# A decoder layer on one core: its last block set apart, the second batch's first chunk normalised earlier, and load buffers divided

## The chip, the cores and the metric

The kernel runs on one core of one Trainium2 chip. The metric is the device time of one execution in microseconds (us), the median of several runs; less is better. The engines are called as in the profile: PE (TensorE, matmuls; PEld its weight loads), DVE (VectorE), ACT (ScalarE), POOL (GpSimd) and SP (SyncE), whose queue here issues all DMAs.

## The reference

Two sequences (B = 2) of 2048 rows and 512 columns go through one decoder layer, in float32:

```python
x = x + _L0_attn_ref(_layernorm(x), W_q, W_k, W_v, W_o)   # 16 heads of 32, rotary positions on Q and K, softmax
x = x + _L0_xattn_ref(_layernorm(x), ctx, ctx)            # gelu(x @ ctx.T) @ ctx, ctx is 77 x 512
x = x + _L0_ffn_ref(_layernorm(x), weights, scale, bias)  # sign(weights), scale, bias, clip to +-100
```

The layer norms have no learned parameters. The attention is over all 2048 keys.

## The kernel before

The rows of a sequence are cut into 16 chunks of 128 rows; four chunks are a block of 512. For each batch two stages follow one another.

**Projection** (`project_batch`). For each chunk the rows are loaded (`load_x`, L69), normalised (`norm`: statistics on DVE, L129 and L130; four small operations on POOL, L135 to L139; the normalised `xn` on ACT, L155), transposed on PE and copied (`turn`: `pt` L161, `xnt` L163), and multiplied by three weights (`pk`, `pq`, `pv`, L168). K and Q are rotated on DVE (L196 to L200) and POOL (L201) and transposed again (`ptqk`, L176). The loop works one chunk ahead: in the round of chunk ch, `norm(ch + 1)` is issued, and its load was issued two chunks ahead. The x tiles of the projection and of the work behind the attention share one pool of six buffers (`xpool`).

**Attention** (`Attention.run`). A unit is a group of four heads with 256 queries; there are 32 units (`NU`) of 8 steps (`STEPS`) in a batch. Each step has two half-steps of two heads each: scores (`st`, L496), exponentials on ACT (`pw`, L623), their pairwise sum on POOL (`sm`, L625). In between come the weighing of the values (`acc`, L514) and the sums (L528) for the step before, and the maxima of the scores for a unit ahead (`ps` L403 on PE, L415 on DVE). The queries' maxima enter the scores as a row `mrow` (L481). `divide` (L542 to L551) ends a unit. Keys are kept as differences from one block to the next; the differences `dk` lie in the buffers of the three projection weights, so that the next batch's weights (`load_qkv`, L74) can be loaded only when the last scores have read them.

**Background.** When a block of queries is done, `divide` puts a generator `after_attention` on a queue. It does the rest of the layer for its chunks: output projection (`po`, L309) and addition to x (L285), normalisation (L292, `xn` L297, transposes `pt` L303), the product with the context (`ph` L316), gelu (L318 to L330), the product back (`po`, L335), normalisation, and the last product (`pf`, L343) with scale, bias, clip, addition and store (L345 to L352). At each `yield` it gives back control and says whether the next piece is heavy, which mostly means matmuls. `background(n)` runs n pieces; with `light=True` it stops ahead of a heavy one. It is called once or twice in each attention step and twice, with three pieces, for each chunk of the projection. The last block of queries is handed over in two halves of two chunks. In batch 1 the second half has one generator for each chunk, and these run when the attention is over, with DVE in POOL's place (`side`).

**Order.** Inside `run`, `tc.manual_schedule` keeps PE, DVE, ACT and POOL in the order in which the program is written. Elsewhere, and for SP everywhere, a scheduler orders the instructions by readiness and place in the program. Each engine and SP's queue then runs in order.

Of the kernel before, what the change touches and what calls it, by code (L numbers as in the profile page):

```python
# [9 lines left out]
F32 = mybir.dt.float32  # L10
# [25 lines left out]
def decoder_layer(  # L36
# [17 lines left out]

    const = ctx.enter_context(tc.tile_pool(name="const", bufs=1))
    kvq = ctx.enter_context(tc.tile_pool(name="kvq", bufs=1))
    xpool = ctx.enter_context(tc.tile_pool(name="xpool", bufs=6))
    big = ctx.enter_context(tc.tile_pool(name="big", bufs=3))
    sums = ctx.enter_context(tc.tile_pool(name="sums", bufs=3))
    work = ctx.enter_context(tc.tile_pool(name="work", bufs=5))  # L60
# [3 lines left out]
    ps_acc = ctx.enter_context(tc.tile_pool(name="ps_acc", bufs=1, space=bass.MemoryType.PSUM))  # L64


    def load_x(b, ch):
        t = xpool.tile([P, D], F32, tag="x", name=f"x_{b}_{ch}")
        nc.sync.dma_start(t, x[b, ch * P : (ch + 1) * P, :])  # L69
        return t  # L70

# [58 lines left out]
        nc.vector.bn_aggr(mv, st)  # L130


    def scale_and_shift(engine, mv, n):
        y = small.tile([P, n], F32, tag=f"rstd{n}", name="rstd")
        engine.tensor_scalar(y, mv[:, :, 1], EPS, None, ALU.add)  # L135
        nc.gpsimd.tensor_tensor(y, y, minus_half[:, :n], ALU.pow)
        off = small.tile([P, n], F32, tag=f"off{n}", name="off")
        engine.tensor_mul(off, mv[:, :, 0], y)
        engine.tensor_scalar(off, off, -1.0, None, ALU.mult)  # L139
        return y, off  # L140

    def project_batch(b, ahead, att, wk, wq, wv):

        def norm(ch):
            xc = ahead.pop(0)
            if ch + 2 < NCH:
                ahead.append(load_x(b, ch + 2))  # L150
            mv = small.tile([P, 1, 2], F32, tag="mv1", name="mv")
            chunk_stats(xc, mv[:, 0])
            y, off = scale_and_shift(nc.gpsimd, mv, 1)
            xn = work.tile([P, D], F32, tag="w", name="xn")
            nc.scalar.activation(xn, xc, AF.Identity, bias=off, scale=y)  # L155
            return xn

        def turn(xn):
            pt = ps_t.tile([P, ND, P], F32, tag="t", name="pt")
            for i in range(ND):  # L160
                nc.tensor.transpose(pt[:, i, :], xn[:, i * P : (i + 1) * P], ident)  # L161
            xnt = work.tile([P, ND, P], F32, tag="w", name="xnt")
            nc.scalar.copy(xnt, pt)  # L163
            return xnt

        def times(dst, xnt, w, part=range(ND)):
            for i in part:
                nc.tensor.matmul(dst, xnt[:, i, :], w[:, i, :], start=(i == 0), stop=(i == ND - 1))  # L168
# [31 lines left out]
            nc.vector.tensor_tensor(t2[:, :, :, 1], pairs[:, :, :, 0], sn, ALU.mult)  # L200
            nc.gpsimd.tensor_add(r[:, 0, a], r[:, 0, a], r[:, 1, a])  # L201

        xnt = turn(norm(0))
        held = None
        for ch in range(NCH):
            if ch == (NB - 1) * CPB:
                drain()
            blk, c = divmod(ch, CPB)
            if c == 0:
                att.q.append(kvq.tile([P, ND, BLK], F32, tag=f"q{blk}", name=f"q_{b}_{blk}"))  # L210
                att.k.append(kvq.tile([P, ND, BLK], F32, tag=f"k{blk}", name=f"k_{b}_{blk}"))
            r = big.tile([P, 2, 2, D], F32, tag="s", name="r")
            xn = norm(ch + 1) if ch + 1 < NCH else None
            pk = ps_t.tile([P, D], F32, tag="t", name="pk")
            pq = ps_t.tile([P, D], F32, tag="t", name="pq")
            if ch == NCH - 1:
                break
            times(pk, xnt, wk)
            rotate(ch, 1, pk, r)
            att.lead(1)  # L220
            background(3)
            times(pq, xnt, wq)
            rotate(ch, 0, pq, r)
            if held is not None:
                transpose_qk(*held)
            held = (ch, r[:, 0])
            xnt_next = turn(xn)
            if ch < NCH - 2:
                values(ch, xnt)
            else:  # L230
                left = xnt
            att.lead(1)
            background(3)
            xnt = xnt_next


# [31 lines left out]
        return ps_t.tile(shape, F32, tag="t", name=name)  # L268


    def after_attention(b, blk, ot, first, end):
        wo, wf, fs, fb = late["wo"], late["wf"], late["fs"], late["fb"]
        ctxn, ctxt = late["ctx"]
        n = end - first
        chunks = [slice(c * P, (c + 1) * P) for c in range(first, end)]
        whole = slice(first * P, end * P)
        xs = [load_x(b, blk * CPB + c) for c in range(first, end)]
        yield True


        def add_to_x(matmuls, mv):
            for c in range(n):
                ps = bank([P, D], "po")
                matmuls(ps, chunks[c])
                nc.vector.tensor_add(xs[c], ps, xs[c])  # L285
                yield False
                chunk_stats(xs[c], mv[:, c, :])
                yield c + 1 < n


        def norm(mv):
            y, off = scale_and_shift(side(), mv, n)  # L292
            yield False
            yield False
            for c in range(n):
                xn = work.tile([P, D], F32, tag="w", name="xn2")
                nc.scalar.activation(  # L297
                    xn, xs[c], AF.Identity, bias=off[:, c : c + 1], scale=y[:, c : c + 1]
                )
                yield True  # L300
                pt = bank([P, ND, P], "pt2")
                for i in range(ND):
                    nc.tensor.transpose(pt[:, i, :], xn[:, i * P : (i + 1) * P], ident)  # L303
                nc.scalar.copy(ot[:, :, chunks[c]], pt)
                yield c + 1 == n
# [2 lines left out]
            for i in range(ND):  # L308
                nc.tensor.matmul(ps, ot[:, i, cols], wo[:, i, :], start=(i == 0), stop=(i == ND - 1))  # L309

        mv = small.tile([P, n, 2], F32, tag=f"mv{n}", name="mv2")
        yield from add_to_x(project_out, mv)
        yield from norm(mv)
        ph = bank([C, n * P], "ph")
        for i in range(ND):
            nc.tensor.matmul(ph, ctxt[:, i, :], ot[:, i, whole], start=(i == 0), stop=(i == ND - 1))  # L316
        h = work.tile([C, n * P], F32, tag="w", name="h")
        nc.scalar.copy(h, ph)  # L318
        yield False
        u = work.tile([C, n * P], F32, tag="w", name="u")  # L320
        side().tensor_mul(u, h, h)
        yield False
        side().tensor_scalar(u, u, 0.044715, 1.0, ALU.mult, ALU.add)
# [10 lines left out]
        def attend_ctx(ps, cols):  # L334
            nc.tensor.matmul(ps, u[:, cols.start - whole.start : cols.stop - whole.start], ctxn, start=True, stop=True)  # L335

        mv = small.tile([P, n, 2], F32, tag=f"mv{n}", name="mv3")
        yield from add_to_x(attend_ctx, mv)
        yield from norm(mv)
        for c, cols in enumerate(chunks):  # L340
            pf = bank([P, D], "pf")
            for i in range(ND):
                nc.tensor.matmul(pf, ot[:, i, cols], wf[:, i, :], start=(i == 0), stop=(i == ND - 1))  # L343
            y = work.tile([P, D], F32, tag="w", name="y")
            nc.vector.tensor_mul(y, pf, fs)  # L345
            yield False
            side().tensor_add(y, y, fb)
            yield False
            side().tensor_scalar(y, y, -MAX_VAL, MAX_VAL, ALU.max, ALU.min)
            side().tensor_add(xs[c], xs[c], y)  # L350
            r0 = blk * BLK + (first + c) * P
            nc.sync.dma_start(out[b, r0 : r0 + P, :], xs[c])  # L352
            yield True

    queue = []
    heavy = [False]

    def background(n, light=False):  # L360
        while queue and n > 0 and not (light and heavy[0]):
            more = next(queue[0], queue)
            if more is queue:
                queue.pop(0)
                heavy[0] = False
            else:
                heavy[0] = more
                n -= 1

    def drain():  # L370
        while queue:
# [5 lines left out]
    class Attention:  # L377
# [160 lines left out]
        def divide(self, u):  # L538
# [16 lines left out]
                )  # L555
            if g == ND - 1 and (hf == 1 or qb == NB - 1):
                first = hf * (CPB // 2) if qb == NB - 1 else 0
                size = 1 if last else (hf + 1) * (CPB // 2) - first
                for c in range(first, (hf + 1) * (CPB // 2), size):
                    queue.append(after_attention(self.b, qb, self.q[qb], c, c + size))  # L560


        def open_block(self, kb):
# [11 lines left out]
        def run(self):  # L575
# [33 lines left out]
            )  # L609
            ordered.__enter__()  # L610
            attending.append(True)
            for t in range(NU * STEPS):
                u, i = divmod(t, STEPS)
                pw = big.tile([P, 4, 2, HQ], F32, tag="s", name="pw")
                sm = sums.tile([P, 4, HQ], F32, tag="sm", name="sm")
                for heads, others in (((0, 1), (2, 3)), ((2, 3), (0, 1))):
# [18 lines left out]
                    else:  # L635
# [6 lines left out]
                            self.turn_maxima(u + 1)  # L642
                        background(1)
                prev = (u, i, pw, sm)
            first_half()
            second_half()
            while ends:
                finish()
            attending.clear()
            ordered.__exit__(None, None, None)  # L650

    for b in range(B):
        att = Attention(b)
        project_batch(b, x_next, att, *qkv)
        if b == 0:
            late_loads()
        load_ctx(b)
        att.run()
        if b + 1 < B:
            x_next = [load_x(b + 1, 0), load_x(b + 1, 1)]  # L660
            qkv = load_qkv()
    alone.append(True)
    while queue:
        for piece in list(queue):
            if next(piece, queue) is queue:
# [47 lines left out]
```

## Time and profile before

| | |
|---|---|
| median of 3 runs | 2783.71 us (2783.66 to 2784.01) |
| the profiled execution, its own time | 2784.56 us |
| its span in the profile | 2782.8 us |
| mean granted clock of PE | 0.996 |
| busy: PE, DVE, ACT, POOL | 99%, 60%, 47%, 63% of the span |

The profile is of one execution. Its span is what the trace covers; the execution's own time is 1.8 us longer. A row of instructions gives line, engine, operation, output and inputs; behind the bar stand busy time, mean duration and idle time ahead with what ended it. A row of waits gives who waited for whom, the total, the number of times and the longest. In a timeline the columns are start and duration in us, then the instruction; matmuls in float32 count as two each.

### The profile page before, as it was taken

To read this page: it belongs to the slowest core of one execution; us is meant where nothing else is said; L and a number is where in the kernel's file an instruction comes from. 1 tells how busy PE (TensorE), PEld (TensorE's weight loads), DVE (VectorE), ACT (ScalarE), POOL (GpSimd) and SP (SyncE) were. 2 spreads that over 40 slices of the span, in tenths; PEclk is the share of its full clock that TensorE was granted. 3 is DMA by queue.
4 is the path that set the end of the run, shared out by engine and by line. 5 is a ranking of instruction groups with operands and counts; after the bars stand their busy time and mean duration, and the time that the engine had idled before them with its cause. 6 is when DMAs were issued, how large, how long until landed. Compare 5 with 4: busy or idle time off the path is not lost.

```text
span 2782.8 us, 70154 instructions
## 1 busy us (share of the span) xinstructions
PE 2750.7 (99%) x30748; PEld 1491.3 (54%) x30748; DVE 1675.7 (60%) x2792; ACT 1320.4 (47%) x2391; POOL 1756.4 (63%) x1903
## 2 busy tenths in 40 slices
PE   8999999999999999999999999999999999999997
PEld 4445555555555555555444455555555555555554
DVE  3436777676666666665234367766757666666652
ACT  2114555455545554654321155555555455545552
POOL 3226767567756685777542277766777567756764
PEclk9999999999999999999999999999999999999999
DMA  4000000000000000000210000000000000000000
GB/s 141 19 16 2 5 4 4 4 4 19 19 4 4 10 27 3 4 19 18 69 31 27 15 4 4 4 4 4 4 24 14 4 4 15 22 3 4 22 7 16
DMA packets 41858, 43.52 MB, mean 16 GB/s; under 512 B 24758, under 2 KB 24758, under 8 KB 41552
## 3 DMA queue, kind: packets, MB, share of 16 engines
q1 hardware_dynamic: 41552, 39.05, 4.7%
q8 instruction: 240, 3.93, 0.6%
q14 instruction: 66, 0.54, 0.1%
HBM read 26.58 MB, written 8.39 MB: 13 GB/s over the span
## 4 chain that ended last, share of the span: by engine, by line
PE 97%; POOL 1%; DVE 1%; DMA 0%; ACT 0%; issue 0%; ACTq 0%; POOLq 0%; DVEq 0%
PE st L496 22%; PE acc L514 22%; PE ps L403 18%; PE acc L528 8%; PE po L309 4%; PE pf L343 4%; PE pq L168 4%; PE pk L168 4%; PE pv L168 4%; PE st L481 3%; PE pt L303 1%; PE po L335 1%; PE ph L316 1%; PE ptqk L176 1%; PE pt L161 1%
## 5 line engine op out<-in xcount | busy, mean ns | idle before, releaser
L625 POOL TENSOR_TENSOR sm<-pw 128x512 f32<-128x512 f32 x1024 | 1296.6, 1271 | 634.5 <-ACT pw L623 631.8
L415 DVE TENSOR_REDUCE mx<-ps 128x1 f32<-128x512 f32 x2048 | 1310.3, 681 | 582.0 <-PE ps L403 579.5
L623 ACT ACTIVATE pw<-st 128x512 f32<-128x512 f32 x2048 | 1111.8, 595 | 1001.8 <-PE ps L403 668.8
L403 PE MATMUL ps<-k,q 32*128 32x512 f32 x4096 | 1208.8, 640 | 1.6 <-DVE mx L415 1.6
L514 PE MATMUL acc<-pw,v 128*32 128x256 f32 x8192 | 655.6, 391 | 0.0
L528 PE MATMUL acc<-sm,ones 128*32 128x128 f32 x7680 | 389.0, 280 | 0.0
L403 PEld LDWEIGHTS ps<-k,q 32*128 32x128 f32 x4096 | 355.3, 183 | 37.7 <-issue 25.8
L514 PEld LDWEIGHTS acc<-pw,v 128*32 128x32 f32 x8192 | 162.4, 108 | 396.3 <-issue 376.6
L528 PEld LDWEIGHTS acc<-sm,ones 128*32 128x32 f32 x7680 | 247.4, 110 | 153.9
L496 PE MATMUL st<-q,dkk 32*128 32x256 f32 x2048 | 291.1, 400 | 0.0
L496 PE MATMUL st<-q,dkq 32*128 32x256 f32 x2048 | 289.9, 400 | 0.0
L496 PE MATMUL st<-q,dkv 32*128 32x256 f32 x2048 | 289.9, 400 | 0.0
L496 PE MATMUL st<-q,k 32*128 32x256 f32 x2048 | 262.8, 374 | 0.0
L201 POOL TENSOR_TENSOR r<-r 128x512 f32<-128x512 f32 x64 | 82.1, 1282 | 246.6 <-DVE r L200 246.3
L496 PEld LDWEIGHTS st<-q,dkk 32*128 32x128 f32 x2048 | 175.4, 184 | 93.2 <-issue 52.3
L496 PEld LDWEIGHTS st<-q,dkq 32*128 32x128 f32 x2048 | 172.7, 184 | 82.6 <-issue 56.7
L496 PEld LDWEIGHTS st<-q,dkv 32*128 32x128 f32 x2048 | 174.7, 184 | 65.2 <-issue 33.6
L496 PEld LDWEIGHTS st<-q,k 32*128 32x128 f32 x2048 | 195.2, 187 | 14.2
L548 DVE RECIPROCAL num<-num 128x128 f32<-128x128 f32 x128 | 120.2, 941 | 60.8 <-ACT num L542 60.8
L177 ACT COPY q<-ptqk 128x512 f32<-128x512 f32 x32 | 18.8, 587 | 232.5 <-PE ptqk L176 232.5
L168 PE MATMUL pk<-wk,xnt 128*128 128x512 f32 x256 | 120.7, 615 | 2.7 <-ACT xnt L163 2.7
L168 PE MATMUL pq<-wq,xnt 128*128 128x512 f32 x256 | 120.9, 612 | 0.0
(90 smaller groups left out, 1860.7 us busy)
## 6 DMA issues: line engine op xcount, KB each, us to landing
x<-in_x_dram SPq DMA_DIRECT2D x64, 256.0 KB, 2.7
out_dram<-x SPq DMA_DIRECT2D x32, 256.0 KB, 2.0
wk<-in_wk_t_dram SPq DMA_DIRECT2D x2, 1024.0 KB, 5.5
wq<-in_wq_t_dram SPq DMA_DIRECT2D x2, 1024.0 KB, 10.5
wv<-in_wv_t_dram SPq DMA_DIRECT2D x2, 1024.0 KB, 9.7
wo<-in_wo_t_dram SPq DMA_DIRECT2D x1, 1024.0 KB
wf<-in_wf_t_dram SPq DMA_DIRECT2D x1, 1024.0 KB, 9.8
mrow<-mt SPq DMA_TRANSPOSE x62, 2.3
```

The costliest lines, as they stand in the source:

```text
L168: nc.tensor.matmul(dst, xnt[:, i, :], w[:, i, :], start=(i == 0), stop=(i == ND - 1))
L309: nc.tensor.matmul(ps, ot[:, i, cols], wo[:, i, :], start=(i == 0), stop=(i == ND - 1))
L343: nc.tensor.matmul(pf, ot[:, i, cols], wf[:, i, :], start=(i == 0), stop=(i == ND - 1))
L403: nc.tensor.matmul(ps, self.q[qb][self.rows[h], g, q0 : q0 + P], self.k[kb][self.rows[h], g, :], start=True, stop=True,)
L415: nc.vector.tensor_reduce(mx[:, qc, h, kb : kb + 1], ps, AX.X, ALU.max)
L481: nc.tensor.matmul(self.st[h], ones_b[r, :], mrow[r, None, :].to_broadcast([DK, 2, HQ]), start=True, stop=False, skip_group_check=True,)
L496: nc.tensor.matmul(self.st[h][:, c, :], keys[r, g, kc * P : (kc + 1) * P], self.q[qb][r, g, hf * HQ : (hf + 1) * HQ], start=False, stop=Tr ...
L514: nc.tensor.matmul(acc[self.rows[h], 0, :], self.v[self.chunk(i, c)][:, d0 : d0 + DK], pw[:, h, c, :], start=(i == 0 and c == 0), stop=(i ...
L528: nc.tensor.matmul(acc[self.rows[h], 1, part], ones, sm[:, h, part], start=False, stop=(i == STEPS - 1), skip_group_check=True,)
L548: nc.vector.reciprocal(num[:, 1, part], num[:, 1, part])
L623: nc.scalar.activation(pw[:, h], self.st[h], AF.Exp, scale=SCALE)
L625: nc.gpsimd.tensor_add(sm[:, hs, :], pw[:, hs, 0, :], pw[:, hs, 1, :])
```

## The change

1. The x tiles get two pools: `xpool` with two buffers for the projection, `xlate` with four for `after_attention`. In the projection the load of chunk ch + 2 is issued behind the normalisation of chunk ch.
2. `norm` and `turn` are no longer local to `project_batch`. The first chunk of batch 1 is loaded in the last unit of batch 0's attention, normalised at the beginning of the last step but one (step 254 of 0 to 255), and transposed behind the last step, before the last weighing.
3. In the projection, `background(3)` at two places for each chunk becomes `background_between(2)` at three: a heavy piece, if it is due, and then light ones, two pieces in all.
4. In batch 1 all four chunks of the last block of queries get generators of their own. They go to a list `tail`, which is worked through in turn when the attention is over.
5. These take their work tiles from the three weight buffers, cut into twelve slices.
6. Mean, variance, scale and shift of a normalisation lie in one tile of four columns.

```diff
-    xpool = ctx.enter_context(tc.tile_pool(name="xpool", bufs=6))
+    xpool = ctx.enter_context(tc.tile_pool(name="xpool", bufs=2))
+    xlate = ctx.enter_context(tc.tile_pool(name="xlate", bufs=4))
...
+    def scale_and_shift(engine, stats):
+        y, off = stats[:, :, 2], stats[:, :, 3]
+        engine.tensor_scalar(y, stats[:, :, 1], EPS, None, ALU.add)
+        nc.gpsimd.tensor_tensor(y, y, minus_half[:, : stats.shape[1]], ALU.pow)
+        engine.tensor_mul(off, stats[:, :, 0], y)
         engine.tensor_scalar(off, off, -1.0, None, ALU.mult)
...
+    def norm(ahead, b, ch):
+        xc = ahead.pop(0)
+        stats = stats_tile(1)
+        chunk_stats(xc, stats[:, 0, 0:2])
+        y, off = scale_and_shift(nc.gpsimd, stats)
+        xn = work.tile([P, D], F32, tag="w", name="xn")
+        nc.scalar.activation(xn, xc, AF.Identity, bias=off, scale=y)
+        if ch + 2 < NCH:
+            ahead.append(load_x(b, ch + 2))
+        return xn
...
             times(pk, xnt, wk)
             rotate(ch, 1, pk, r)
             att.lead(1)
-            background(3)
+            background_between(2)
             times(pq, xnt, wq)
             rotate(ch, 0, pq, r)
+            background_between(2)
...
             att.lead(1)
-            background(3)
+            background_between(2)
...
+    def work_tile(shape, name):
+        if not alone:
+            return work.tile(shape, F32, tag="w", name=name)
+        if not spare:
+            for n in "kqv":
+                t = const.tile([P, ND, D], F32, tag=f"w{n}", name=f"spare{n}")
+                spare.extend(t[:, i, :] for i in range(ND))
+        t = spare.pop(0)
+        spare.append(t)
+        return t[: shape[0], : shape[1]]
...
-        xs = [load_x(b, blk * CPB + c) for c in range(first, end)]
+        xs = [load_x(b, blk * CPB + c, xlate) for c in range(first, end)]
...
+    def background_between(n):
+        if heavy[0]:
+            background(1)
+            n -= 1
+        background(n, light=True)
...
-                size = 1 if last else (hf + 1) * (CPB // 2) - first
+                late = self.b == B - 1 and qb == NB - 1
+                size = 1 if late else (hf + 1) * (CPB // 2) - first
                 for c in range(first, (hf + 1) * (CPB // 2), size):
-                    queue.append(after_attention(self.b, qb, self.q[qb], c, c + size))
+                    (tail if late else queue).append(
+                        after_attention(self.b, qb, self.q[qb], c, c + size)
+                    )
...
+            more = self.b + 1 < B
             for t in range(NU * STEPS):
                 u, i = divmod(t, STEPS)
+                if more and t == (NU - 1) * STEPS:
+                    self.x_next = [load_x(self.b + 1, 0), load_x(self.b + 1, 1)]
+                if more and t == NU * STEPS - 2:
+                    xn = norm(self.x_next, self.b + 1, 0)
...
+            xnt = turn(xn) if more else None
             first_half()
             second_half()
...
     alone.append(True)
+    queue += tail
     while queue:
         for piece in list(queue):
```

## The prediction

> **What bounds the kernel now.** I read the page's busy shares first, then who PE waited for, then PE's busy time and granted clock in windows of 50 us and less, then the timeline where PE was not full.
>
> ```profile
> PE 2750.7 (99%) x30748; PEld 1491.3 (54%) x30748; DVE 1675.7 (60%) x2792; ACT 1320.4 (47%) x2391; POOL 1756.4 (63%) x1903
> PE pt L161 <- ACT xn L155: 9.5, 2, 8.1
> PE pt L303 <- ACT xn L297: 8.1, 5, 3.6
> PE pk L168 <- ACT xnt L163: 2.7, 4, 0.7
> PE po L335 <- DVE u L330: 2.3, 1, 2.3
> PE ps L403 <- DVE mx L415: 1.6, 1, 1.6
> ```
>
> PE is the bound; it idles 2782.8 - 2750.7 = 32.1 us. By the windows: 8.8 before the first matmul, 2.1 where the projection of batch 1 follows the attention of batch 0 (1363 to 1366), 2.1 at 1380 to 1400, 1.6 at 1466 to 1468, 14.3 after 2750, the rest in pieces below 1.1. Only these, and PE's work itself, can be shortened. Some of the idle stretches also cost clock:
>
> ```profile
> 1466.00:1469.00 3.00, 1.39 (x3) 0.82 0.00 0
> 1469.00:1472.00 3.00, 3.00 (x4) 0.50 0.00 0
> 1363.00:1366.00 3.00, 1.14 (x5) 0.92 1.01 363
> 1366.00:1369.00 3.00, 3.00 (x4) 0.51 0.41 141
> 2760.00:2765.00 5.00, 2.50 (x4) 0.66 0.00 0
> 2765.00:2770.00 5.00, 3.63 (x10) 0.50 0.00 0
> ```
>
> (Columns: window, length, PE busy and count, granted clock, DMA.) After each gap PE runs at half clock for 3 to 5 us.
>
> **A. Last block moved to the end.** Of batch 1's last block, chunks 0 and 1 ran as background of the last four units; now all four chunks run alone. First, what leaves the attention:
>
> ```profile
> 2710.91 1.13 PE L496 MATMUL st<-q,dkk 32*128 32x256 f32 x8
> 2712.54 3.70 PE L343 MATMUL pf<-wf,q 128*128 128x512 f32 x8
> 2716.17 1.13 PE L496 MATMUL st<-q,dkq 32*128 32x256 f32 x8
> 2718.02 1.13 PE L496 MATMUL st<-q,dkq 32*128 32x256 f32 x8
> 2719.87 1.13 PE L496 MATMUL st<-q,dkv 32*128 32x256 f32 x8
> ```
>
> A half-step takes 1.85 us (2716.17 to 2718.02); with a pf in it 5.26 to 5.48 us: the piece costs its full 3.63 (2712.54 to 2716.17). [...] The cadence decides: they aren't free. Pieces by the same reading: 2 po and 2 pf at 3.63, 4 pt at 0.59, ph 1.88, 2 ctx products (L335) at 1.06: 14.5 + 2.4 + 1.9 + 2.1 = 20.9 us leave. POOL (1.27 per half-step), ACT (1.09) and DVE stay below 1.85, so no other engine becomes the bound there.
>
> Second, the end. Before, it runs from 2744.6 (first po) to 2782.8, 38.2 us for two chunks: PE's work, 5.7 us behind the last pf (2777.1: multiply, add, clip, add on DVE 2.6, store 2.0 and the rest) and 8.6 us of holes. After: PE's work per chunk is po 3.54, pt 0.60, ph 1.11, L335 1.06, pt 0.60, pf 3.63 = 10.5 alone; packed, as in the projection where four matmuls take 3.43, about 9.7. I take 10.2, so 40.8 for four. The holes are one chunk's latency: po's end to ph is 5.2 us (add 0.69, statistics 0.69, POOL's power 0.56, xn 0.81, transposes 0.66, copy 0.59 and gaps), ph to L335 2.3 to 4.7, then 5 again. With four chunks, behind the last po stand the others' pt, ph and L335, some 8 us of PE work, which cover 5 us; the last pf waits behind three others (10 us). What cover leaves out: about 1 us before the first pf, and DVE. DVE's work per chunk is 2 adds, 2 statistics, 2 sets of small ones (0.18 + 0.15 + 0.16 + 0.15), 1.3 for the gelu and 2.5 at the end: 7.8, four times 31.3, with reciprocals and gaps some 37 us in the 46 that it has. At 80% its queue makes PE wait; I put holes at 2.5 and lost clock at 1.0. End: 40.8 + 3.5 + 5.7 = 50.0, 11.8 more. **A: -20.9 + 11.8 = -9.1** (end holes between 0 and 9 make it -12.6 to -3.6).
>
> Its DMAs: four loads, four stores. The first two loads move from the background to SP's position behind everything, but into four buffers that block 2 has left (its last pf is at 2635.9), and SP has only two transposes and the stores then, so they land long before 2744. Only the last store is seen, within the 5.7. The twelve slices of the dead weight buffers as work tiles cost nothing (dk's last reader is the last scores, before 2744), nor do statistics, scale and shift in one tile: as many instructions as before, and though the tile is now held until xn is read, so is the x buffer.
>
> **B. Load buffers apart.** At 1466 PE stands for this:
>
> ```profile
> 1460.87 0.34 SPq L352 DMA_DIRECT2D out_dram<-x  x1
> 1462.86 0.81 SPq L69 DMA_DIRECT2D x<-in_x_dram  x2
> 1465.62 1.38 DVE L129 BATCH_NORM_STATS2 st<-x 128x6 f32<-128x512 f32 x2 [2.11 <-DMA x<-in_x_dram]
> 1467.64 1.81 PE L403 MATMUL ps<-k,q 32*128 32x512 f32 x2 [1.61 <-DVE mx L415]
> ```
>
> The projection's x waits for a buffer that a background chunk frees only when its store has landed (1462.86); the statistics then hold DVE, DVE the maxima, these PE's bank: 1.61 us, and the next pq takes 6.29 in the chain instead of 3.43: 2.86 more. With two buffers of its own the load waits for the normalisation of the chunk before instead: ACT's xn, then issue 0.3, landing 2.7, statistics 0.9, POOL 1.2, xn 0.8: 6 us in a period of 11 to 13. Behind the waiting load on SP stand the stores and the other loads, which nobody needs soon. The load can still queue behind a store waiting for POOL, but not for its landing (2.0), more than the 1.61. **B: -4.5** (0 if it is still late).
>
> [...] The gaps of 1.61 here, and of 1.40 and 0.68 at 1363, brought 0.50 and 0.51. [...]
>
> **C. Background spread out** (at most one heavy piece per place, three places per chunk). At 1391.38 PE waits 2.10 for xn of the background, since scale, xn and transposes follow too closely. Now places with 3 to 4 us of matmuls lie between. **C: -2.1** (0 to -2.1). The 34 pieces take 22 places, 7 to 8 chunks; the drain before chunk 12 finds nothing.
>
> **D. First chunk of batch 1 in the first attention.** Moved into step 254: two DVE and four POOL instructions, xn on ACT; then four transposes and a copy before the last weighing; two x loads earlier on SP, a third before the weights. Before, from the end of acc (1362.84) to the end of pk (1370.91) pass 8.1 us, 3.4 of it work, 0.66 transposes. But POOL is late:
>
> ```profile
> 1351.48 1.27 POOL L350 TENSOR_TENSOR x<-x,y 128x512 f32<-128x512 f32 x1
> 1352.71 6.19 POOL L625 TENSOR_TENSOR sm<-pw 128x512 f32<-128x512 f32 x5
> 1354.18 1.09 ACT L623 ACTIVATE pw<-st 128x512 f32<-128x512 f32 x2 [0.82 <-PE st L496]
> ```
>
> Before step 254's exponentials (1354.18) three of the five sums precede in POOL's order, so its four small operations start near 1356.4 and take 1.4; xn ends near 1358.7. ACT runs in order: the exponentials, and PE's next scores behind them, are late by 4.6, of which 1.4 is slack: PE stands about 3 us, acc ends near 1365.9, pk follows at once, ending 1369.3 at full clock or 1371.3 at half. The weights, behind the third x load on SP, land 5.5 us after 1359.1: in time. Bounds: -4.0 (no delay) to +1.5. **D: -0.6**, the middle of the two clocks.
>
> **Sum.** -9.1 - 4.5 - 2.1 - 0.6 = -16.3. The profiled execution: span 2782.8, 1.8 around it, 2784.6, which is 0.9 above the median 2783.7. I subtract from the median: 2767.4.
>
> **Rivals.** (1) Lockstep: the four generators, taken in turn, put the in-order queues in stage order, and each stage waits for its last chunk. End: po 14 + 5.2 + 2.4 + gelu 5 + 1 + 5 + 1.3 + pf 14 + 5.7 = 53.6, and 4 for the clock, 57.6: +19.4, A -1.5, total -8.7: 2775. For: DVE at 80%. Against: before, DVE took chunk 2's chain whole before chunk 3's add. (2) It does not happen: the scheduler pulls the ready chunks back into the attention, as it did with batch 1's first statistics (at 1315, 47 us before their use). Then A is 0: -7.2, 2776.5. Against: no matmul was pulled ahead. (3) Slower: the background was free in PE's shadow[...]. Then the attention gives back nothing, the end costs 11.8, B to D give 7.2: +4.6, 2788. It decides when less than 4.6 of the 20.9 is given back. Against: 3.63 for 3.63. (4) Better: POOL is not late at D and the end packs: -4.0 and -11 with B and C: 2762.
>
> **How the numbers follow.** Main forecast 0.62 (2761 to 2773), lockstep 0.15, pulled back 0.09, free background 0.06, better 0.08. The measurement tells 0.2% (5.6 us, below 2778.1) from no change: faster is 0.62 + 0.08 + 0.12 + 0.05 = 0.87, within 0.07, slower 0.06. The range 2758 to 2777 takes in the better case, most of lockstep and half of (2).
>
> **What would show it.** The last units of batch 1 without pf, their half-steps 1.85; PE from the first lone po to the last pf about 44 us at clock near 1; no PE wait for mx near 1466 and none for L297 near 1391; a PE wait of about 3 us on exponentials near 1357, and none between acc and pk. Wrong: an end above 56 us, or po, pf inside the last unit, or the attention shortened by much less than 20.

## The result, and the profile after

The changed kernel takes 2774.64 us (2772.49 to 2775.69, 7 runs) against 2783.71 (2780.70 to 2784.57, 7 runs): a ratio of 0.9967, with a 95% interval of 0.9956 to 0.9979, so 6 to 12 us less. The profiled execution took 2774.21 us, its span is 2772.1. The forecast was 2767.4, within 2758 to 2777.

The busy shares and the waits of PE after (a row of waits: who waited for whom, total, times, longest):

```profile
PE 2746.3 (99%) x30756; PEld 1493.4 (54%) x30756; DVE 1682.3 (61%) x2820; ACT 1320.7 (48%) x2393; POOL 1745.2 (63%) x1888
PE pt L161 <- ACT xn L153: 8.2, 1, 8.2
PE pt L321 <- ACT sparek L315: 4.9, 3, 4.1
PE st L523 <- ACT pw L658: 3.1, 1, 3.1
PE pk L171 <- ACT xnt L163: 2.0, 3, 0.7
PE acc L555 <- POOL sm L660: 0.6, 1, 0.6
PE po L353 <- DVE sparev L348: 0.5, 1, 0.5
```

Three of the waits of before are gone: those of ps for mx, of the background's pt for xn, and of batch 1's first pt for xn (L161 now waits once, at the start of the program). New ones are there: `st` for the exponentials, 3.1, `acc` for a sum of POOL, 0.6, and `pt` in the end for xn, 4.9 (`sparek` is a work tile of the end). The first two lie in the last steps of batch 0's attention, where before PE waited for nothing.

Where the time went is seen best between points that all kernels share: the first maxima row of batch 0's step 252, batch 1's first pk, the first scores of batch 1's attention, the first po behind the attention, the end of the span. Each is the start of one row in the timeline of PE. Each line is one profiled execution; the same stage of the same program differs by up to 1.8 us between lines (the end with unchanged code: 52.2 to 53.8). Stage lengths in us:

| kernel | step 252 to pk | pk to attention of batch 1 | attention of batch 1 | the end | span |
|---|---|---|---|---|---|
| before | 20.2 | 241.5 | 1137.6 | 38.2 | 2782.8 |
| after | 26.4 | 231.7 | 1116.8 | 52.2 | 2772.1 |
| e1, first chunk back | 20.2 | 233.4 | 1117.3 | 53.8 | 2770.0 |
| e2, at step 250 | 17.5 | 231.8 | 1116.9 | 52.5 | 2766.9 |
| e3, small operations at 250 | 18.7 | 231.8 | 1117.2 | 52.3 | 2765.7 |
| e4, two chunks left out | 20.2 | 239.7 | 1117.4 | 40.1 | 2763.5 |
| e5, end alone | 20.2 | 235.4 | 1116.9 | 52.9 | 2771.0 |
| e6, pools alone | 20.2 | 235.5 | 1137.5 | 38.2 | 2777.9 |
| e7, spread alone | 20.2 | 235.3 | 1137.6 | 38.3 | 2777.8 |
| e8, gelu of the end on POOL | 26.3 | 231.8 | 1116.8 | 57.6 | 2777.1 |
| e9, end staggered | 25.9 | 231.7 | 1116.9 | 51.2 | 2769.8 |
| e10, e3 and staggered | 18.8 | 231.7 | 1116.9 | 51.9 | 2764.5 |
| e11, one tile alone | 20.2 | 235.4 | 1137.8 | 38.6 | 2777.4 |

From before to after: +6.2 up to pk, -9.8 in the projection, -20.8 in the attention, +14.0 at the end, and 0.4 earlier at step 252: -10.7, the difference of the spans. In the first two stages 1.7 us only change places: pk ran at half clock before (5.39 us) and at full clock after (3.70). Counted to the end of pk, the first stage is 4.5 longer and the projection 8.1 shorter.

The stage that went wrong is the first. Around step 254 of batch 0 the timeline after shows, in order:

```profile
1345.36 0.23 POOL L139 TENSOR_SCALAR stats<-stats 128x1 f32<-128x1 f32 x1 [0.41 <-DVE stats L131]
1353.76 3.72 POOL L660 TENSOR_TENSOR sm<-pw 128x512 f32<-128x512 f32 x3
1357.56 0.23 POOL L139 TENSOR_SCALAR stats<-stats 128x1 f32<-128x1 f32 x1
1359.08 0.81 ACT L153 ACTIVATE xn<-x,stats 128x512 f32<-128x512 f32 x1 [6.13 <-POOL stats L142]
1359.80 2.04 ACT L658 ACTIVATE pw<-st 128x512 f32<-128x512 f32 x4
1360.43 2.56 PE L523 MATMUL st<-q,dkv 32*128 32x256 f32 x8 [3.09 <-ACT pw L658]
1371.33 3.70 PE L171 MATMUL pk<-wk,xnt 128*128 128x512 f32 x8
```

Three sums hold POOL until 1357.5, its four small operations follow, xn comes at 1359.08, and the exponentials, for which the scores were long ready, only at 1359.80 (ACT stood 6.13 us). PE waits 3.09. POOL was late for one more reason: a set of small operations already stands at 1345.36 to 1349.31. It must be chunk 1's, since chunk 0's xn waits for the later set. Chunk 1's normalisation stands behind `run` in the program; the scheduler put this part of it here, ahead of chunk 0's, and POOL's sums are 1.5 us later against step 252 than in the kernel before. The windows, cut where the granted clock changes, show what the wait does to the clock (window, length, PE busy and count, granted clock, DMA); the last one is in the end:

```profile
1356.50:1359.92 3.42, 0.84 (x18) 1.00 0.92 264
1359.92:1370.16 10.24, 9.73 (x72) 0.50 0.71 239
2745.73:2752.56 6.83, 3.75 (x17) 0.50 0.00 0
```

From 1359.92 to 1370.16 PE runs at half clock, busy for 9.73 us of it, so that 4.9 us are lost: the two half-steps of step 255, the transposes and the last weighing take about twice their time (scores 2.56 and 2.08 instead of 1.13). pk then starts directly behind acc and at full clock.

The attention gives back what was forecast; its last half-steps keep 1.85, and the end begins with four po at once:

```profile
2713.81 1.13 PE L523 MATMUL st<-q,dkv 32*128 32x256 f32 x8
2715.66 1.13 PE L523 MATMUL st<-q,dkv 32*128 32x256 f32 x8
2719.88 14.00 PE L327 MATMUL po<-wo,q 128*128 128x512 f32 x32
```

(No pf stands among them; a half-step is still 2715.66 - 2713.81 = 1.85.) In the end itself the hole lies between the last context product and the second normalisation of chunk 0 (x_12 in the program):

```profile
2741.69 0.68 DVE L303 TENSOR_TENSOR x<-po,x 128x512 f32<-128x512 f32 x1
2743.83 0.68 DVE L130 BATCH_NORM_STATS2 st<-x 128x6 f32<-128x512 f32 x1
2744.59 0.69 DVE L303 TENSOR_TENSOR x<-po,x 128x512 f32<-128x512 f32 x1
2745.20 0.17 DVE L131 BATCH_NORM_AGGREGATE stats<-st 128x2 f32<-128x6 f32 x1
2748.65 1.12 PE L321 MATMUL pt<-ident,sparek 128*128 128x128 f32 x4 [4.10 <-ACT sparek L315]
2752.55 13.91 PE L361 MATMUL pf<-wf,q 128*128 128x512 f32 x32
```

Chunk 0's addition ends at 2742.4; its statistics start 1.4 us later, behind the gelu and the additions of the others, and the aggregate waits in DVE's order behind the fourth addition (2744.59). DVE has no room in this stretch (window, length, DVE busy and count, granted clock of PE, DMA):

```profile
2737.80:2747.80 10.00, 9.71 (x38) 0.90 0.00 0
```

So two things delay chunk 0: DVE is full, and its order serves the other chunks first.

### The profile page after: what moved, and what is told of

Read it like the earlier page. It is cut to its first block, busy times and chain, and to the rows that moved or that the text cites. A ratio compares the mean times of both kernels' runs of the same rounds, so it can differ in the third digit from the quotient of the medians.

```text
span 2772.1 us, 70180 instructions
## 1 busy us (share of the span) xinstructions
PE 2746.3 (99%) x30756; PEld 1493.4 (54%) x30756; DVE 1682.3 (61%) x2820; ACT 1320.7 (48%) x2393; POOL 1745.2 (63%) x1888
## 4 chain that ended last, share of the span: by engine, by line
PE 98%; DVE 1%; POOL 1%; issue 0%; ACT 0%; DMA 0%; POOLq 0%; ACTq 0%; DVEq 0%
PE st L523 22%; PE acc L541 22%; PE ps L430 18%; PE acc L555 8%; PE pk L171 4%; PE pf L361 4%; PE po L327 4%; PE pq L171 4%; PE pv L171 4%; PE st L508 3%; PE pt L321 1%; PE po L353 1%; PE ptqk L179 1%; PE ph L334 1%; PE pt L161 1%
## 5 line engine op out<-in xcount | busy, mean ns | idle before, releaser
L180 ACT COPY q<-ptqk 128x512 f32<-128x512 f32 x32 | 18.8, 587 | 218.7 <-PE ptqk L179 218.6
```

## The experiments

The theory after the result: the attention returned A's 20.9 us as forecast; the shortfall lies in D, whose late POOL costs more than was taken, and in the end, whose hole is larger than taken. Rivals: the pieces in the attention were partly free; D is harmless and all of the shortfall is in the end; xn in front of the exponentials is harmful wherever it stands. The kernel before was measured again beside the runs, with medians of 2784.46 to 2785.27 us, so the ratios are compared and not the times.

**e4: are the pieces free?** From the kernel before; batch 1's first half block gets no work behind the attention.

```diff
+                if self.b == B - 1 and qb == NB - 1 and hf == 0:
+                    return
                 size = 1 if last else (hf + 1) * (CPB // 2) - first
```

> The kernel before, but with the work behind the attention left out for batch 1's last block, first half (chunks 0 and 1; their rows of the output are not computed). It asks what these pieces cost in the attention. Theory (PE is full, each piece costs its whole time): 20.9 us less, 2763 us. Rival (the pieces were free in PE's shadow[...]): 2780 or more, less than 5 us saved.

Measured 2763.93 us against 2785.27, ratio 0.9924 (0.9910 to 0.9937). The attention of batch 1 is 20.2 us shorter in the trace (1117.4 for 1137.6), and 20.8 in the changed kernel. The pieces cost their whole time; the rival falls. The projection of batch 1 is 1.8 us shorter here than in the kernel before, though its program is the same; a half-clock stretch behind the same wait for mx lasted 3.41 us in place of 6.83 (the windows stand in the last section). That is how much one execution's clock can be worth.

**e1: D undone.** The loads of chunks 0 and 1 and `turn(norm(...))` stand again behind `run`.

```diff
-                if more and t == (NU - 1) * STEPS:
-                    self.x_next = [load_x(self.b + 1, 0), load_x(self.b + 1, 1)]
-                if more and t == NU * STEPS - 2:
-                    xn = norm(self.x_next, self.b + 1, 0)
...
-            xnt = turn(xn) if more else None
...
-        project_batch(b, x_next, att, xnt, *qkv)
+        project_batch(b, x_next, att, turn(norm(x_next, b, 0)), *qkv)
```

> The changed kernel with part D alone undone: batch 1's first chunk is again loaded, normalised and transposed behind batch 0's attention; pools, spread background and the end stay as changed. Theory (D costs 4.4 us by the traces: a PE wait of 3.1 on the exponentials of step 254 and some 10 us at half clock behind it): about 2770 us, 4 to 5 less than the changed kernel, no wait of st for pw, pt waiting 1.4 for xn and pk 0.7 for xnt again. Rival (D is neutral or a gain, and the shortfall against the forecast lies in the end): 2774 to 2779.

Measured 2771.87 us, 0.9954 (0.9941 to 0.9966) of before; the changed kernel has 0.9967 (0.9956 to 0.9979). The intervals overlap, so the times alone don't settle it; the stages do: from step 252 to the attention of batch 1 pass 253.6 us with D undone and 258.2 with it. D costs 4.5 us. The end took 53.8 here, 1.6 more than in the changed kernel, with the same code and the same waits: 1.1 is half clock that fell on more work (the four pf take 15.01 for 13.91), the rest lies behind the last pf.

**e2: the same step earlier.**

```diff
-                if more and t == (NU - 1) * STEPS:
+                if more and t == (NU - 2) * STEPS:
...
-                if more and t == NU * STEPS - 2:
+                if more and t == NU * STEPS - 6:
```

> The changed kernel with the normalisation of batch 1's first chunk issued at step 250 instead of 254 (its loads one unit earlier). POOL is idle near that step in the trace of before (1333 to 1336.7). Theory (the harm of D is POOL's lateness at step 254, not the move as such): no PE wait for exponentials, pk directly behind acc at full clock, so about 4 us better than the form of before: 2766 us. Rival (any xn put among the exponentials delays them, since ACT runs in order): a wait stays, 2770 or more.

Measured 2770.67 us, 0.9948 (0.9936 to 0.9961). The expectation failed: a wait stays, and the time is above 2770, as the rival had it. Step 252 to pk falls to 17.5, but PE waits 1.9 for exponentials already at step 251, and half clock follows there (the next pf takes 5.40 for 3.70). From the second maxima row of step 248 to the end of pk pass 46.5 us before, 51.0 after, 46.3 in e2: nothing is won against the kernel before. The rival's reason is tested in e3. The timeline shows another engine than I had looked at:

```profile
1333.33 0.69 DVE L363 TENSOR_TENSOR y<-pf,fs 128x512 f32<-128x512 f32 x1 [5.14 <-PE pf L361]
1333.93 1.28 DVE L130 BATCH_NORM_STATS2 st<-x 128x6 f32<-128x512 f32 x2
1335.38 0.23 POOL L139 TENSOR_SCALAR stats<-stats 128x1 f32<-128x1 f32 x1 [3.49 <-DVE stats L131]
1337.48 0.81 ACT L153 ACTIVATE xn<-x,stats 128x512 f32<-128x512 f32 x1 [7.35 <-POOL stats L142]
1338.83 1.61 PE L523 MATMUL st<-q,dkv 32*128 32x256 f32 x8 [1.91 <-ACT pw L658]
```

POOL is idle, as foreseen (3.49), but DVE stands 5.14 for a background pf, and the statistics behind it. The statistics are those of two chunks (x2): chunk 1's were put here too and stand between chunk 0's links on DVE and POOL. The chain through three in-order engines is late at another link.

**e3: the small operations early, xn late.** `norm` takes a finished scale and shift; the statistics and POOL's operations are issued at step 250, xn at step 254.

```diff
+                if more and t == NU * STEPS - 6:
+                    stats = stats_tile(1)
+                    chunk_stats(self.x_next[0], stats[:, 0, 0:2])
+                    ready = scale_and_shift(nc.gpsimd, stats)
                 if more and t == NU * STEPS - 2:
-                    xn = norm(self.x_next, self.b + 1, 0)
+                    xn = norm(self.x_next, self.b + 1, 0, ready)
```

> The changed kernel with the move divided: the statistics on DVE and the four POOL operations at step 250, the normalisation itself (ACT) still at step 254. Theory (POOL's lateness): xn takes its 0.8 us on ACT and no more; the slack of 1.4 us between a step's exponentials and the next scores covers it: 2766 to 2767 us, wait of st for pw below 0.5. Rival (xn on ACT in front of the exponentials is what delays them): the wait of about 3 us stays and the time with it, 2774.

Measured 2768.07 us, 0.9940 (0.9927 to 0.9952), its interval just below the changed kernel's. The wait for exponentials is gone from the list of PE's waits (one of 0.8 for a sum of POOL stays), the stretch from step 248 falls to 43.4 us, and the timeline has xn in the gap between two steps' exponentials:

```profile
1353.58 0.81 ACT L155 ACTIVATE xn<-x,stats 128x512 f32<-128x512 f32 x1
1354.52 1.09 ACT L664 ACTIVATE pw<-st 128x512 f32<-128x512 f32 x2
```

So xn in front of the exponentials is harmless if its inputs are there; what it waited for was the harm. The expected 2766 to 2767 was missed by 1.

**e5, e6, e7 and e11: A, B, C and the sixth part each alone.** e5 is the changed kernel with D undone and one x pool of six, the load ahead of the normalisation, and `background(3)` at two places; e11 is e5 with the tail undone too. e6 and e7 start from the kernel before:

```diff
# e6 (the load is also moved behind the normalisation)
-    xpool = ctx.enter_context(tc.tile_pool(name="xpool", bufs=6))
+    xpool = ctx.enter_context(tc.tile_pool(name="xpool", bufs=2))
+    xlate = ctx.enter_context(tc.tile_pool(name="xlate", bufs=4))
...
# e7
-            background(3)
+            background_between(2)
             times(pq, xnt, wq)
             rotate(ch, 0, pq, r)
+            background_between(2)
...
-            background(3)
+            background_between(2)
```

> Part A alone (with the statistics in one tile, without which the buffers don't fit): batch 1's last block as four generators at the end, one x pool of six buffers, background(3), first chunk of batch 1 behind the attention. Theory (A is -20.8 in the attention, +14.0 at the end by the traces): 6.7 us less than before, 2777 to 2778. Rival (the end is dearer without the pools apart, or the attention gives back more): outside 4 to 9 us.

> Part B alone: two x buffers for the projection and four for the rest, the load behind the normalisation. Theory: the wait of ps for mx near 1467 (1.6) and the half clock behind it (2.9) go: 4.5 us less than before; no PE wait for mx. Rival (the load is still late behind a store on SP, or the gain of the projection was all from the spread background): 0 to 2 us less.

> Part C alone: the background spread over three places for each chunk of the projection, one pool of six. Theory: the wait of pt for xn near 1391 (2.1) goes, the late x load stays: 2 us less than before. Rival (spreading also moves the stores and so the buffer that the x load waits for): 6 us or more less, without B, or none since the late load strikes elsewhere.

> The sixth part alone: mean, variance, scale and shift in one tile, with the kernel before in all else (one x pool of six, background(3), two chunks of the last block in the attention). It asks why e5, which has neither B nor C, lost the wait for mx in the projection all the same. Theory (the statistics' tile is now held until xn is read, which moves the statistics on DVE and with them the place where a late x load strikes): 5 to 6 us less than before, no PE wait for mx. Rival (the part does nothing by itself, e5's gain came with the end): time as before, the wait for mx of 1.6 there.

Measured: e5 2773.03 us, 0.9958 (0.9946 to 0.9971) of before; e6 2779.62, 0.9980 (0.9971 to 0.9989); e7 2779.62, 0.9984 (0.9976 to 0.9991); e11 2779.73, 0.9981 (0.9973 to 0.9989). e6 came out at the expected size. e5 saved 11.4 instead of 6.7, and e11 says why: 5.2 of it is the sixth part, so that A alone is worth 6.2. e7 saved 4.8, more than its 2. The waits of PE between 1360 and 1610, first in e11, then in e7:

```profile
PE pt L320 <- ACT xn L314: 2.1, 1, 2.1
PE pt L161 <- ACT xn L155: 1.4, 1, 1.4
PE pk L171 <- ACT xnt L163: 1.3, 2, 0.7
```

```profile
PE pt L161 <- ACT xn L155: 1.4, 1, 1.4
PE pk L168 <- ACT xnt L163: 1.4, 2, 0.7
PE ps L410 <- DVE mx L422: 1.3, 1, 1.3
```

e11 has lost the wait for mx, though its x tiles still share one pool; the background's wait of 2.1 stays, as in e6. e7 has lost the 2.1, and keeps the wait for mx (1.3). All of e5, e6, e7 and e11 have 235.3 to 235.5 us from pk to the attention, 6.1 less than before, but not for one reason. In e6 and e11 1.6 is the wait, 3.4 the half clock behind it (6.83 us of it before) and about 1 less work of PE. In e7 3.4 is clock that fell more kindly, with pk at full clock and half clock of 3.42 us in place of 6.83 behind the wait for mx, which is still there; its own part is some 2.8, near the 2 expected. B and the sixth part remove the same wait, so their gains don't add; C's comes on top, and together (e1) they save 8.1.

That e6's buffers did what they were meant for is not so. First the kernel before, then e6:

```profile
1454.83 0.69 DVE L129 BATCH_NORM_STATS2 st<-x 128x6 f32<-128x512 f32 x1 [4.25 <-DMA x<-in_x_dram]
1455.44 0.67 DVE L345 TENSOR_TENSOR y<-pf,fs 128x512 f32<-128x512 f32 x1
```

```profile
1453.38 0.69 DVE L346 TENSOR_TENSOR y<-pf,fs 128x512 f32<-128x512 f32 x1 [2.05 <-PE pf L344]
1458.84 0.34 SPq L353 DMA_DIRECT2D out_dram<-x  x1
1460.84 0.81 SPq L70 DMA_DIRECT2D x<-in_x_dram  x2
1464.14 0.69 DVE L130 BATCH_NORM_STATS2 st<-x 128x6 f32<-128x512 f32 x1 [5.38 <-DMA x<-in_x_dram]
```

In e6 a pair of loads still goes out 2.0 us behind a store, the time that the store took to land (before: 1460.87 and 1462.86), and the statistics still wait for x, 5.38. What changed is the order of DVE. Before, the background's y (from pf) stands behind statistics that wait 4.25 for x; in e6 it stands ahead of them. So the store that follows from it goes out 3.3 us sooner, counted from pk (92.1 for 95.4), and the load behind it too. In e11, with one pool, it is the same (92.0). The timeline shows this chain; that one tile held longer is what turned the order round in e11 is not shown, since each of these runs changes the order as a whole.

**e8: is DVE too full in the end?** The five gelu operations of the end go to POOL.

```diff
-        side().tensor_mul(u, h, h)
+        nc.gpsimd.tensor_mul(u, h, h)
...
-        side().tensor_scalar(u, u, 1.0, 0.5, ALU.add, ALU.mult)
-        side().tensor_mul(u, u, h)
+        nc.gpsimd.tensor_scalar(u, u, 1.0, 0.5, ALU.add, ALU.mult)
+        nc.gpsimd.tensor_mul(u, u, h)
```

> The changed kernel with the five gelu operations of the end on POOL, which is idle there, instead of DVE. Theory (the hole of 4.1 us in the end is DVE's queue: the gelu of chunks 2 and 3 and all four additions stand ahead of chunk 0's second statistics): the hole shrinks to 2 or less and the half clock behind it with it, 2 to 4 us less than the changed kernel. Rival (the hole is the latency of one chunk's chain): it stays at 4, or grows since POOL is slower, time the same or more.

Measured 2779.10 us, 0.9982 (0.9973 to 0.9990): the interval overlaps the changed kernel's a little, but the stage is clear, with an end of 57.6 for 52.2. The gain that my theory expected did not come. With DVE relieved of 20 operations the hole is as long as before:

```profile
2742.49 0.69 DVE L303 TENSOR_TENSOR x<-po,x 128x512 f32<-128x512 f32 x1 [6.13 <-PE po L353]
2743.21 0.69 DVE L130 BATCH_NORM_STATS2 st<-x 128x6 f32<-128x512 f32 x1
2748.41 0.69 DVE L303 TENSOR_TENSOR x<-po,x 128x512 f32<-128x512 f32 x1 [1.57 <-PE po L353]
2749.02 0.17 DVE L131 BATCH_NORM_AGGREGATE stats<-st 128x2 f32<-128x6 f32 x1
2752.47 1.12 PE L321 MATMUL pt<-ident,sparek 128*128 128x128 f32 x4 [4.17 <-ACT sparek L315]
```

Chunk 0's statistics end at 2743.9; the aggregate, 0.17 us of work, comes at 2749.02, since the order of DVE puts it behind the fourth chunk's addition, which waits for PE, which waits for POOL's slower gelu (0.45 for a product that takes DVE 0.28). DVE is busy for only 6.05 of the 15.07 us from 2737.40 to 2752.47, so in this run order and the slower gelu make the hole. For the changed kernel, where DVE is full at that place, the run does not tell load and order apart: it moved the load to a slower engine on the same path.

**e9: the end staggered.** Generator k starts 4k rounds later.

```diff
+    starts = [0, 4, 8, 12]
+    rounds = 0
     while queue:
-        for piece in list(queue):
-            if next(piece, queue) is queue:
-                queue.remove(piece)
+        for k, piece in enumerate(list(tail)):
+            if piece in queue and rounds >= starts[k]:
+                if next(piece, queue) is queue:
+                    queue.remove(piece)
+        rounds += 1
```

> The changed kernel with the four generators of the end started 4 pieces apart instead of together; the work is the same. Theory (the hole of 4.1 us in the end is stage order: on DVE chunk 0's second statistics stand behind the additions of all four chunks, and so behind PE's last ctx product): the hole falls below 2 us, the end from 52.2 to 48 to 50 us, 2 to 4 us less than the changed kernel. Rival (the hole is latency that four chunks can't cover, it only moves to the last chunk): the end stays at 52 or more, no gain.

Measured 2773.48 us, 0.9960 (0.9946 to 0.9974); the end 51.2 in place of 52.2. The wait of 4.1 is gone, but others take its place, the largest

```profile
2741.89 0.66 PE L321 MATMUL pt<-ident,sparev 128*128 128x128 f32 x4 [2.69 <-ACT sparev L315]
```

for chunk 2's first normalisation, now behind the second ones of chunks 0 and 1. Holes in the middle of the end fall from 5.4 to 4.2 us by the list of waits. Less than expected: a part of the hole was order, the rest moved. The gain in time is not shown, since the intervals of the two ratios overlap and 1.0 us is less than the end varies with the same code.

**e10: e3 and e9 together.**

> Both mends together: statistics and POOL operations of batch 1's first chunk at step 250 with xn at step 254 (as in e3), and the end started 4 pieces apart (as in e9). Theory: the two lie in different stages and add up, e3's 17 us less than before and 2 to 4 more: 2764 to 2766 against 2784.5. Rival: the staggered end gives nothing, 2767 to 2768.

Measured 2765.09 us, 0.9932 (0.9919 to 0.9944) of before: the fastest here, clearly ahead of the changed kernel; against e3 the intervals overlap, and the stage (51.9 for 52.3) gives the stagger 0.4, which is within what the end varies. The gain shown is e3's.

## Why the prediction was right, and where it was not

The time lay in the range and the direction was right; the gain was little more than half of the forecast (9.1 of 16.3 us by the medians, 10.7 by the spans). Two terms were too hopeful, D by 5.1 and the end by 2.2; B, C and the sixth part gave 1.5 more than forecast. That lockstep's total (2775) is the one measured is chance: its end is 5.4 too long, and it leaves D as it was.

- **A, the attention: right.** 20.9 forecast, 20.8 measured, 20.2 in e4. The cadence of half-steps was the right view, and with it rival 3 fell; the busy share of 99% pointed the same way.
- **A, the end: the term for holes mis-sized.** 50.0 forecast, 52.2 measured. PE's work was over-estimated (40.8; first po to the end of the last pf is 46.6, less 5.4 of holes and 1.9 of clock leaves 39.3), what follows the last pf was 5.7 as forecast, but holes were 5.4 instead of 2.5 and the clock 1.9 instead of 1.0. The failing step is "what cover leaves out: about 1 us before the first pf, and DVE": I reasoned from work that was available, but the order written for DVE holds chunk 0 back until chunk 3 has caught up. That is rival 1's mechanism: PE did go stage by stage, but only one stage waited long, so rival 1's price (57.6) was too high. The reading "at 80% its queue makes PE wait" was right in kind: at the hole DVE is 97% busy (9.71 of 10.00 us). Its 80% is an average over the end and hid this.
- **B: right in size, by luck.** The wait and the half clock went, 4.8 us by the medians for 4.5 forecast. The step "but not for its landing" failed: in e6 the load still follows a store's landing, and the wait went because DVE's order changed. e11 shows that the sixth part, costed at nothing, takes the same wait away; "as many instructions as before" says nothing of what a longer-held tile may do to the order.
- **C: right.** The 2.1 us are gone in e7 and in the changed kernel; the rest of e7's gain is mostly clock. B, C and the sixth part together gave 8.1 for the 6.6 forecast.
- **D: the step that failed.** -0.6 forecast, +4.5 measured, outside its bounds of -4.0 to +1.5. The chain came as described: late POOL, late xn, a wait of 3.1 us for 3, pk directly behind acc. The size of the wait was partly luck: POOL's four operations came 1.6 us later than forecast (1357.56 for 1356.4, with step 252 0.4 earlier), through chunk 1's operations, and the slack was larger than 1.4. What failed is "1369.3 at full clock or 1371.3 at half". I took half clock to last "3 to 5 us" and to fall on pk alone, about 1 us on the mean; it lasted 10.24 us, fell on the half-steps behind the gap, and cost 4.9, while pk ran at full clock. Smaller terms are missing too: the four transposes moved ahead of the last weighing (0.6) and the wait for a sum (0.6). The trace of before could have warned: its half clock lasts 6.83 us behind the wait for mx and 10.24 in the end, not 3 to 5, and behind the wait of 2.1 at 1391 there is none.
- **Rival 2** (pulled back into the attention) did not happen: the attention has the shorter length in every kernel with the new end.

## What to carry to other kernels

A small step moved into a full pipeline is not free because its engines are idle on average: follow its chain link by link through each in-order queue at that very place, and put in front only what has its inputs already (`st` waits 3.1 us for the exponentials in the changed kernel and 1.9 in e2; in e3 that wait is gone). A gap of 1.3 to 3.1 us on the bound PE mostly cost itself and 3.4 to 10.2 us of half clock on whatever came next (1.3 and 3.4 in e7, 3.1 and 10.2 in the changed kernel; a gap of 2.1 in the kernel before cost itself alone). When several parts remove the same wait, measure them apart before adding their gains, and look in the trace whether the wait went in the way that was meant. When chains are taken in turn, look at the engine that they share just where the hole is: at how full it is there (DVE 97% here), not on average, and at what its order puts first.

## What the runs showed of the hardware

Half clock behind a gap lasted longer than the prediction took from the trace of before, and its lengths repeat. The stretches of it that end within the trace last 3.41 us (before, e1, e4, e5, e6, e7), 6.83 (before, after, e1, e2, e3, e5), 10.24 (before, after, e6, e7, e8) and 13.7 (e8): one, two, three and four times 3.41. The full clock between two of them lasts 98.98 us before (1368.96 to 1467.94) and 17.06 after (2752.56 to 2769.62): 29 and 5 times 3.41, to within 0.1 us. Four windows show half clock, cut at the changes: the kernel before at its first pk and behind the wait for mx, e4 behind the same wait, e7 behind its wait for mx.

```profile
1365.54:1368.96 3.42, 3.42 (x4) 0.50 0.50 174
1467.94:1474.77 6.83, 6.83 (x9) 0.50 0.00 0
1469.11:1472.52 3.41, 3.41 (x5) 0.50 0.00 0
1480.22:1483.64 3.42, 3.42 (x5) 0.50 0.02 5
```

The same waits did not always have the same price. Those of 1.4 and 0.7 ahead of batch 1's first pk brought pk to 5.26 to 5.40 us in before, e1, e4, e5, e6 and e11, and left it at 3.70 in e7. The windows below are 3.41 us long and counted back from the next stretch of half clock. Before, both waits fall into one of them; in e7 one ends within the first wait:

```profile
1362.12:1365.54 3.42, 1.35 (x13) 1.00 1.05 360
1360.80:1364.21 3.41, 3.02 (x56) 1.00 1.07 390
1364.21:1367.62 3.41, 1.72 (x7) 1.00 0.94 336
```

Behind the first of these lines the clock fell to 0.50, behind the other two it stayed at 1.00. That the place of the waits made the difference is an estimate from these lines; it was not tested. PE's busy share in such a window does not alone decide: one of the kernel before with only 1.47 us busy (1389.44 to 1392.85) was followed by full clock, one with 1.81 (1464.52 to 1467.94) by half. What decides, and how many times 3.41 us the half clock lasts, stays open.

Single waits of 1.3, 1.6 and 1.9 us were followed by half clock (e7, before, e2). 3.41 us at half clock, more or less, is 1.7 us of PE's work: pk took 3.70 us in e7 for 5.39 before, and the projection of e4, with 3.41 us behind the wait for mx in place of 6.83, 239.7 for 241.5. That is as much as several of the steps that were forecast.
